# Marks, steps and relative nodes of two edge chunks in PSUM, and a pair's three lists joined by one reduction

## The chip, the cores and the metric

The kernel runs on one core of a Trainium2 chip. The metric is the device time of one execution in microseconds (us). The kernel before takes 1126.28 us, the median of three runs (1125.23 to 1130.48).

## What is computed

A layer of a graph network on 12,500 nodes with 128 features and 400,000 edges. The edges come sorted by their destination `dst`; the sources are random. An edge that is longer than 10 contributes nothing (`cut` is 0 there), and `edge_weight` is scaled so that most edges are longer. The reference, cut to what matters:

```python
rbf = exp(-(distances[:, None] - centers) ** 2 / (2 * width * width))       # 50 centers
cut = 0.5 * (cos(pi * distances / CUTOFF) + 1) * (distances <= CUTOFF)
W = (silu(rbf @ fw1 + fb1) @ fw2 + fb2) * cut[:, None]
messages = (h[src] @ pw + pb) * W
agg = segment_sum(messages, dst, num_segments=num_atoms)
y = h + (silu(agg @ mw1 + mb1) @ mw2 + mb2)
return layernorm(x + y)
```

## The kernel before

The engines are named as in the profile: PE multiplies matrices, DVE and ACT work on tiles, POOL issues the indirect DMAs (gathers and scatters by index), SP issues the plain DMAs.

**The kept edges are packed first.** The edges are cut into seven chunks; chunk c has 128 partitions with `ROWS[c]` edges each (309, 256, then 512). `pack_first` (chunk 0) and `pack(c)` (L660, the others) move each partition's kept edges to the front. For a chunk, `pack` does this on DVE:
- L671 takes the first destination of each partition, L677 marks the edges that are dropped (`drop`), a scan counts the marks along the partition (`gone`), and `step` is that count at the kept edges: by so many places each must move.
- `nodes` puts step, relative destination (`rel`, L713 or L725) and source into one 32-bit word. `spans` (L701, with L703 and L705) finds the largest relative destination. `rank` (L692, with the products L695 and L696) has PE add up the counts of the partitions before.
- For each bit of the largest step, `moving`, `resting` and `shift` (L491, L495, L485) move the edges whose step has that bit: first the words, then the lengths `r_d`.
- `columns` (L434) writes what is kept as lines, and POOL scatters them into a list in DRAM (`packed`, L470). Ahead of the fifth bit step, from chunk 2 on, SP loads the rows of the next chunk (`load_rows`, L174 to L181).

From chunk 3 on (`FROM_BANK`, `late_c`) marks, steps and relative nodes take turns in one PSUM bank, `aside`. For chunks 1 and 2 they are three tiles in SBUF, and the marks' scan takes them as both of its inputs.

**Then the list is unpacked.** Neighbouring partitions write into three different lists, so that they do not collide at their ends. `unpack(c)` (L778) loads the three into `pair`, with two 32-bit words for an edge in turn (word 0 the nodes, word 1 the length). `one_of` (L804 to L807) makes one list of the three, 256 edges wide, with two ORs: once for the nodes, once for the lengths, so 14 times in all. At a given place at most one of the three lists is not zero; chunks 0 and 1 have two more lists, which `alike_in` (L800) ORs in ahead. From the joined list come the sources of the gathers (`srci`, L874), the columns (`dl`) and the cut (`cut`); the lengths go to DRAM (`near_d`).

**The main loop** (L1463) works on quads of 512 kept edges, 139 of them. `fetch` (L1009) gathers four times 128 rows of the projected nodes `proj` by `srci` with L1015 on POOL, ahead of their use, into a ring of buffers; eight quads take their first 128 rows in single copies by SP (`one_by_one`, L992 to L1005). `basis`, `first`, `silu` and `second` (L1065 to L1082) compute the weights of the edges on ACT and PE; `message` (L1086, L1093) multiplies gathered rows and weights on DVE; `place` (L1100, L1105) makes a one-hot operand with the cut in it; `sum_up` (L1117, L1125) sums over the edges on PE into the PSUM tile "sums" (two buffers); `add` (L1144, L1148) adds the sum into the table `aggT` at its base. The node part (up to L1232) runs on the finished end of the table and after the loop.

**The order of the work** is written out when the program is built. `pack` and `unpack` are generators: each `yield` gives the modelled cost of what was just issued, and `go_on` and `pack_until` (L1360 to L1376) put packing steps between the quads while the sum of these costs, `clock[0]`, allows it. `fetches` does the same for the gathers. So a `yield` that changes can move instructions behind or ahead of others on every engine. The two costs used are

```python
def one(n):
    return 0.14 + 0.00112 * n
def two_a_cycle(n):
    return 0.13 + 0.0006 * n
```

Of the kernel before, what the change touches and what calls it, by code (L numbers as in the profile page):

```python
# [20 lines left out]
P = 128  # L21
# [4 lines left out]
W = 128  # L26
# [5 lines left out]
SB = 14  # L32
# [48 lines left out]
def kernel(  # L81
# [37 lines left out]
    nc = tc.nc  # L119
# [17 lines left out]
    ps = ctx.enter_context(tc.tile_pool(name="ps", bufs=2, space=PSUM))  # L137
# [114 lines left out]
    ones = keep.tile([P, P], F32, name="ones")  # L252
# [129 lines left out]
    LB = RB + SB  # L382
# [277 lines left out]
    def pack(c):  # L660

        R, CAP = ROWS[c], CAPS[c]
        bits = (R - 1).bit_length()

        def rowed(dt, name, n=R, bufs=1):
            return work.tile([P, max(n, R_MAX) if n == R else max(CAPS)], dt, name=name,
                             bufs=bufs)[:, :n]

        r_d, r_dst, r_src = raw[c]
        first = work.tile([P, 1], F32, name="first")  # L670
        nc.vector.tensor_copy(first, r_dst[:, 0:1])  # L671
        late_c = c >= FROM_BANK
        if late_c:
            aside = bank(c)
            held.append(c)
        drop = aside[:, :R] if late_c else rowed(F32, "drop")
        nc.vector.tensor_scalar(drop, r_d.bitcast(F32), CUTOFF, None, op0=OP.is_gt)  # L677
        yield (one(R) if late_c else two_a_cycle(R)) + 0.1
        gone = rowed(F32, "gone")
        if late_c:  # L680
            nc.vector.tensor_tensor_scan(gone, drop, ones[:, 0:1].to_broadcast([P, R]), 0.0,
                                         op0=OP.add, op1=OP.mult)
        else:
            nc.vector.tensor_tensor_scan(gone, drop, drop, 0.0, op0=OP.add, op1=OP.max)
        yield one(2 * R)
        nc.vector.tensor_scalar(cnt[:, c:c + 1], gone[:, R - 1:R], -1.0, float(R),
                                op0=OP.mult, op1=OP.add)
        step = aside.bitcast(I32)[:, :R] if late_c else rowed(I32, "step")
        nc.vector.scalar_tensor_tensor(step, drop, 0.0, gone, op0=OP.is_equal, op1=OP.mult)
        yield one(R) + 0.1  # L690

        def rank():  # L692
            at = bank()
            held.append(c)
            nc.tensor.matmul(at[:, 0:1], before, cnt[:, c:c + 1], start=True, stop=False)  # L695
            nc.tensor.matmul(at[:, 0:1], ones, run, start=False, stop=True)  # L696
            return at

        nodes = rowed(I32, "nodes", bufs=2)

        def spans():  # L701
            relc = rowed(F32, "drop")
            nc.vector.tensor_scalar(relc, rel, -127.5, None, op0=OP.add)  # L703
            yield two_a_cycle(R)
            nc.vector.tensor_reduce(span[:, c:c + 1], relc, AX.X, OP.max, apply_absolute_value=True)  # L705
            yield one(R)

        if late_c:
            nc.vector.scalar_tensor_tensor(nodes, step, LB, r_src, op0=OP.logical_shift_left,
                                           op1=OP.bitwise_or)  # L710
            yield one(R)
            rel = aside.bitcast(I32)[:, :R]
            nc.vector.tensor_scalar(rel, r_dst, first, None, op0=OP.subtract)  # L713
            yield one(R)
            nc.vector.scalar_tensor_tensor(nodes, rel, SB, nodes, op0=OP.logical_shift_left,
                                           op1=OP.bitwise_or)
            yield one(R)
            yield from spans()
            held.remove(c)
            free.append(aside)  # L720
            at = rank()
        else:
            at = rank()
            rel = rowed(I32, "rel")
            nc.vector.tensor_scalar(rel, r_dst, first, None, op0=OP.subtract)  # L725
            yield two_a_cycle(R)
            yield from spans()
            nc.vector.scalar_tensor_tensor(nodes, rel, SB, r_src, op0=OP.logical_shift_left,
                                           op1=OP.bitwise_or)
            yield one(R)  # L730
            nc.vector.scalar_tensor_tensor(nodes, step, LB, nodes, op0=OP.logical_shift_left,
                                           op1=OP.bitwise_or)
            yield one(R)
        for b in range(bits):
            if b == 4 and 1 < c < NC_ - 1:
                load_rows(c + 1)
            if b == (1 if late_c else 0):
                if 3 not in side_of:
                    sides(3, nc.vector)
                    yield 0.6  # L740
                at_i = place_at(at, side_of[3])
                nc.vector.tensor_add(run, run, cnt[:, c:c + 1])
                held.remove(c)
                free.append(at)
                yield 0.4
# [24 lines left out]
            yield one(n)  # L770

        yield from columns(c, nodes, r_d, first, 0, CAP, at_i)
        awake[c] = pool[0] + (2.2 if c == 1 else 3.0)
        awake[0] = 0.0
        yield 0
        yield from unpack(c)

    def unpack(c):  # L778
# [5 lines left out]
        np_ = p1 - p0  # L784
        pair = work.tile([64, 3, 512], I32, name="pair", bufs=1)
# [17 lines left out]

        def one_of(to, k):  # L804

            nc.vector.tensor_tensor(to, pair[:np_, 0, k::2], pair[:np_, 1, k::2], OP.bitwise_or)
            nc.vector.tensor_tensor(to, to, pair[:np_, 2, k::2], OP.bitwise_or)  # L807

        if c < 2:
            alike_in(0)  # L810
# [11 lines left out]
        two = paired(I32, "two")  # L822
# [834 lines left out]
```

## Time and profile before

| | |
|---|---|
| median of 3 runs | 1126.28 us (1125.23 to 1130.48) |
| the profiled execution | 1136.76 us |
| its span in the profile | 1134.8 us |
| granted PE clock, mean | 0.761 of full speed |
| PE busy, matmuls | 657.0 us (58%) |
| DVE busy | 582.2 us (51%), 1755 instructions |
| POOL busy | 531.7 us (47%) |
| ACT busy | 399.8 us (35%) |
| DMA | 91.38 MB, 81 GB/s over the span |

The span is the time from the first to the last recorded instruction, and 2 us of the profiled execution lie around it. A row of instructions gives their busy time, the mean of one, and the idle time of the engine just ahead of them with what ended it; "quad<-proj,srci" are the tiles written and read, and x407 the count. In lists of waits, the three numbers are the idle time in us, how often, and the longest. A minimum, median and maximum of one instruction stand as a/b/c in ns. In a timeline each row has its start and length in us, and in the bracket the engine's idle time ahead of it and what ended that. A table by stretches gives the busy time of each engine between two moments.

### The profile page before, as it was taken

What the parts mean: (1) busy time and instruction counts of PE and PEld (TensorE: products, weight loads), DVE (VectorE), ACT (ScalarE), POOL (GpSimd) and SP (SyncE); (2) the same over time, 40 slices, a digit from 0 to 9 for tenths busy, and PEclk for the clock granted to TensorE, in tenths of its full rate; (3) what the DMA queues carried; (4) which work ended last, traced back from release to release, by engine and by line L of the source; (5) the groups of instructions that cost most, each with busy time, mean ns of one, the idle gap of its engine ahead of it and who ended that gap; (6) DMA issues with size and microseconds to landing.
All of it is one profiled execution on the core that took longest, in us unless ns stands there. A gap on an engine that the chain in (4) does not pass through costs nothing. (4 is left out here: it accounts for less than half of the span.)

```text
span 1134.8 us, 13638 instructions
## 1 busy us (share of the span) xinstructions
PE 657.0 (58%) x3531; PEld 509.4 (45%) x3531; DVE 582.2 (51%) x1755; ACT 399.8 (35%) x569; POOL 531.7 (47%) x569
## 2 busy tenths in 40 slices
PE   4574337507724577125856557579266667776685
PEld 4463226406513455114645435457145455554464
DVE  8355409514723476135957557348035344444476
ACT  3344213105412245003525423156035234324565
POOL 7434732464274524745061465552745565565400
PEclk8776657858866788557987769589568778788798
DMA  6572231122121222212121223223223222322322
GB/s 213 178 234 79 72 103 39 40 83 68 57 55 44 61 73 70 63 30 68 58 75 39 64 82 92 58 69 107 62 61 98 80 69 61 113 73 76 115 61 78
DMA packets 53104, 91.38 MB, mean 81 GB/s; under 512 B 13824, under 2 KB 20576, under 8 KB 53018
## 3 DMA queue, kind: packets, MB, share of 16 engines
q1 hardware_dynamic: 34610, 53.34, 14.6%
q0 software_dynamic: 17840, 36.77, 12.4%
q8 instruction: 30, 0.49, 0.2%
q14 instruction: 56, 0.46, 0.1%
q10 hardware_dynamic: 568, 0.33, 0.1%
HBM read 74.59 MB, written 15.79 MB: 80 GB/s over the span
## 5 line engine op out<-in xcount | busy, mean ns | idle before, releaser
L1015 POOL DMA_INDIRECT quad<-proj,srci x407 | 387.2, 951 | 329.0 <-DVE msg L1093 116.4
L1082 PEld LDWEIGHTS bank<-fw_sb,s 128*128 128x128 f32 x1112 | 170.9, 218 | 138.8 <-issue 129.8
L1065 PE MATMUL ph<-rbf,w_sb 102*128 102x512 f32 x278 | 167.6, 731 | 91.7 <-ACT s L1071 52.2
L1105 DVE TENSOR_SCALAR hot<-iota_n,dl,cut 128x80 f32<-128x80 f32 (+4 forms) x408 | 110.1, 332 | 206.9 <-remote 110.5
L1071 ACT ACTIVATE s<-ph 128x1024 f32<-128x1024 f32 x70 | 71.3, 1018 | 359.5 <-remote 222.4
L1082 PE MATMUL bank<-fw_sb,s 128*128 128x128 f32 x1112 | 172.9, 302 | 34.9 <-issue 34.9
L1125 PEld LDWEIGHTS sums<-hot,msg 128*128 128x128 f32 x816 | 121.4, 215 | 96.4 <-issue 84.5
L1125 PE MATMUL sums<-hot,msg 128*128 128x80 f32 (+4 forms) x816 | 122.8, 294 | 52.0 <-issue 48.5
L1065 PEld LDWEIGHTS ph<-rbf,w_sb 102*128 102x128 f32 x278 | 57.9, 231 | 142.6 <-issue 74.9
L1079 PE MATMUL bank<-fb_b,ones_b 96*128 96x512 bf16 x139 | 59.1, 425 | 92.6 <-DVE msg L1093 37.8
L1015 POOL DMA_INDIRECT x<-proj,srci x93 | 88.1, 947 | 46.6 <-issue 27.4
L1148 DVE TENSOR_TENSOR aggT<-aggT,sums 128x80 f32 (+4 forms) x209 | 54.0, 258 | 100.4 <-remote 56.4
L327 PEld LDWEIGHTS bank<-pw_sb,xT 128*128 128x128 f32 (+1 forms) x292 | 47.9, 234 | 90.0 <-issue 71.4
L1056 ACT ACTIVATE rbf<-d,rbf_bias,rbf_scale 102x512 f32<-102x512 f32 x70 | 56.3, 804 | 70.2 <-DMA d<-near_d 60.9
L1093 DVE TENSOR_TENSOR msg<-bank,quad 128x512 f32<-128x512 f32 x78 | 52.9, 679 | 34.7 <-remote 24.6
L470 POOL DMA_INDIRECT packed<-line,at_i x7 | 7.0, 996 | 127.4 <-DVE first L671 75.1
L1015 POOL DMA_INDIRECT quad<-in_x_dram,srci x48 | 46.2, 963 | 43.4 <-DMA r_dst<-in_dst_dram 15.7
L324 PE MATMUL bank<-pb_b,ones_b 96*128 96x512 bf16 (+2 forms) x38 | 17.2, 452 | 81.7 <-ACT xT L951 62.9
L1125 PE MATMUL sums<-quad,quad 128*128 128x128 f32 (+3 forms) x296 | 44.8, 290 | 15.6 <-issue 14.9
L951 ACT COPY xT<-bank 128x512 f32<-128x512 f32 (+1 forms) x37 | 21.4, 579 | 91.5 <-remote 76.9
L327 PE MATMUL bank<-pw_sb,xT 128*128 128x128 f32 (+1 forms) x292 | 48.8, 320 | 4.2 <-ACT xT L951 4.2
L1125 PEld LDWEIGHTS sums<-quad,quad 128*128 128x128 f32 x296 | 40.7, 207 | 17.8 <-issue 16.3
(273 smaller groups left out, 920.8 us busy)
## 6 DMA issues: line engine op xcount, KB each, us to landing
d<-near_d SPq DMA_DIRECT2D x70, 256.0 KB
dl<-proj SPq DMA_DIRECT2D x1024, 0.5 KB
x<-in_x_dram SPq DMA_DIRECT2D x46, 256.0 KB
quad<-proj,srci POOLq DMA_INDIRECT x407
proj<-hp SPq DMA_DIRECT2D x24, 256.0 KB
out_dram<-x SPq DMA_DIRECT2D x22, 256.0 KB
x<-proj,srci POOLq DMA_INDIRECT x93
r_d<-in_edge_weight_dram SPq DMA_DIRECT2D x5, 256.0 KB
```

What stands on the lines that cost most here:

```text
L327: nc.tensor.matmul(to[:m, k, :], lT[:, k * P:k * P + m], w, start=False, stop=(k == a + c - 1))
L951: nc.scalar.copy(xT[:, :n], xp[:, :n])
L1015: nc.gpsimd.indirect_dma_start(out=got[:, j, :], out_offset=None, in_=proj if table is None else table, in_offset=bass.IndirectOffsetOnAxi ...
L1056: nc.scalar.activation(rbf[:u], d[:u], AF.Square, bias=rbf_bias[:u], scale=rbf_scale[:u])
L1065: nc.tensor.matmul(ph[:, h, :], w1_sb[:2 * KR, h, :], rbf[:2 * KR], start=True, stop=True)
L1071: nc.scalar.activation(s[:, :n], ph[:, :n], AF.Silu)
L1079: nc.tensor.matmul(pu, ones_b[:, :P], bias_b["fb2"].rearrange("k j f -> k (j f)"), start=True, stop=False)
L1082: nc.tensor.matmul(pu[:, j * H:(j + 1) * H], s[:, j * P:(j + 1) * P], fw2_sb, start=False, stop=(j == QT - 1))
L1093: nc.vector.tensor_mul(msg[:, a:b, :], pu_of[q].rearrange("p (j f) -> p j f", j=QT)[:, a:b, :], got_of[q][:, a:b, :])
L1105: nc.vector.tensor_scalar(hot[:, j, :wide(q)], iota_n[:, :wide(q)], dl[:, at[0], at[1]], cut[:, at[0], at[1]], op0=OP.is_equal, op1=OP.mult)
L1125: nc.tensor.matmul(pa[:, k * W:k * W + wide(q)], msg[:, j, :], hot[:, j, :wide(q)], start=(j % n == 0), stop=(j % n == n - 1))
L1148: nc.vector.tensor_add(to, to, pa[:, k * W:k * W + wide(q)])
```

## The change

Two edits, one on `pack`, one on `one_of`:
- For chunks 1 and 2 `aside` is a buffer of the PSUM tile "sums" (in their time the main loop has not begun to use it; the assertion says so). Marks, steps and relative nodes of all chunks from 1 on now live in `aside`, one after the other, and all take the order that the late chunks had: the words get the steps first, then `rel` is made over the steps and joined in, then `spans`. For chunks 1 and 2 `rank` is still requested ahead of these. The scan takes a broadcast one as its second input for all of them. The modelled cost of the marks' and of `rel`'s step grows from `two_a_cycle(R)` to `one(R)`.
- `one_of` is one reduction by exclusive or along the three lists, in place of two ORs: the view is turned so that the innermost axis runs over the lists.

```diff
@@ pack
+        else:
+            assert "two" not in pa_of
+            aside = ps.tile([P, 2, 2 * W], F32, name="sums", bufs=2).rearrange("p a w -> p (a w)")
-        drop = aside[:, :R] if late_c else rowed(F32, "drop")
+        drop = aside[:, :R]
         nc.vector.tensor_scalar(drop, r_d.bitcast(F32), CUTOFF, None, op0=OP.is_gt)
-        yield (one(R) if late_c else two_a_cycle(R)) + 0.1
+        yield one(R) + 0.1
...
-            nc.vector.tensor_tensor_scan(gone, drop, drop, 0.0, op0=OP.add, op1=OP.max)
+        nc.vector.tensor_tensor_scan(gone, drop, ones[:, 0:1].to_broadcast([P, R]), 0.0,
+                                     op0=OP.add, op1=OP.mult)
...
-        step = aside.bitcast(I32)[:, :R] if late_c else rowed(I32, "step")
+        step = aside.bitcast(I32)[:, :R]
...
+        if not late_c:
+            at = rank()
+        nc.vector.scalar_tensor_tensor(nodes, step, LB, r_src, op0=OP.logical_shift_left,
+                                       op1=OP.bitwise_or)
+        yield one(R)
+        rel = aside.bitcast(I32)[:, :R]
+        nc.vector.tensor_scalar(rel, r_dst, first, None, op0=OP.subtract)
+        yield one(R)
+        nc.vector.scalar_tensor_tensor(nodes, rel, SB, nodes, op0=OP.logical_shift_left,
+                                       op1=OP.bitwise_or)
+        yield one(R)
+        yield from spans()
         if late_c:
...
-        else:
-            at = rank()
-            rel = rowed(I32, "rel")
-            nc.vector.tensor_scalar(rel, r_dst, first, None, op0=OP.subtract)
-            yield two_a_cycle(R)
-            yield from spans()
-            nc.vector.scalar_tensor_tensor(nodes, rel, SB, r_src, op0=OP.logical_shift_left,
-                                           op1=OP.bitwise_or)
-            yield one(R)
-            nc.vector.scalar_tensor_tensor(nodes, step, LB, nodes, op0=OP.logical_shift_left,
-                                           op1=OP.bitwise_or)
-            yield one(R)
@@ one_of
-            nc.vector.tensor_tensor(to, pair[:np_, 0, k::2], pair[:np_, 1, k::2], OP.bitwise_or)
-            nc.vector.tensor_tensor(to, to, pair[:np_, 2, k::2], OP.bitwise_or)
+            nc.vector.tensor_reduce(to, pair[:np_, :, k::2].rearrange("p s e -> p e s"), AX.X,
+                                    OP.bitwise_xor)
```

More of the change, by code (lines that the diff above doesn't have):

```diff
@@ L675, in pack @@
             held.append(c)
-        drop = aside[:, :R] if late_c else rowed(F32, "drop")
+        else:
+            assert "two" not in pa_of
+            aside = ps.tile([P, 2, 2 * W], F32, name="sums", bufs=2).rearrange("p a w -> p (a w)")
+        drop = aside[:, :R]
         nc.vector.tensor_scalar(drop, r_d.bitcast(F32), CUTOFF, None, op0=OP.is_gt)
-        yield (one(R) if late_c else two_a_cycle(R)) + 0.1
+        yield one(R) + 0.1
         gone = rowed(F32, "gone")
-        if late_c:
-            nc.vector.tensor_tensor_scan(gone, drop, ones[:, 0:1].to_broadcast([P, R]), 0.0,
-                                         op0=OP.add, op1=OP.mult)
-        else:
-            nc.vector.tensor_tensor_scan(gone, drop, drop, 0.0, op0=OP.add, op1=OP.max)
+        nc.vector.tensor_tensor_scan(gone, drop, ones[:, 0:1].to_broadcast([P, R]), 0.0,
+                                     op0=OP.add, op1=OP.mult)
         yield one(2 * R)
@@ L706, in spans @@
             yield one(R)
-        if late_c:
-            nc.vector.scalar_tensor_tensor(nodes, step, LB, r_src, op0=OP.logical_shift_left,
-                                           op1=OP.bitwise_or)
-            yield one(R)
-            rel = aside.bitcast(I32)[:, :R]
-            nc.vector.tensor_scalar(rel, r_dst, first, None, op0=OP.subtract)
-            yield one(R)
-            nc.vector.scalar_tensor_tensor(nodes, rel, SB, nodes, op0=OP.logical_shift_left,
-                                           op1=OP.bitwise_or)
-            yield one(R)
-            yield from spans()
+        if not late_c:
[10 more added lines that the diff above has]
+        yield from spans()
+        if late_c:
             held.remove(c)
@@ L721, in pack @@
             at = rank()
-        else:
-            at = rank()
-            rel = rowed(I32, "rel")
-            nc.vector.tensor_scalar(rel, r_dst, first, None, op0=OP.subtract)
-            yield two_a_cycle(R)
-            yield from spans()
-            nc.vector.scalar_tensor_tensor(nodes, rel, SB, r_src, op0=OP.logical_shift_left,
-                                           op1=OP.bitwise_or)
-            yield one(R)
-            nc.vector.scalar_tensor_tensor(nodes, step, LB, nodes, op0=OP.logical_shift_left,
-                                           op1=OP.bitwise_or)
-            yield one(R)
         for b in range(bits):
```

## The prediction

> **What bounds the kernel now.** I read the page first, then the list of waits, then the busy time by stretches, and last the timelines of the stretches in which the change works. "POOL gather" is one L1015 instruction: it fetches 128 rows by index.
>
> ```profile
> span 1134.8 us, 13638 instructions
> ...
> L1015 POOL DMA_INDIRECT quad<-proj,srci x407 | 387.2, 951 | 329.0 <-DVE msg L1093 116.4
> ```
> ```profile
> POOL quad L1015 <- DVE msg L1093: 116.4, 17, 24.7
> ...
> POOL packed L470 <- DVE first L671: 75.1, 3, 35.6
> ```
> ```profile
> core 0: us, PE busy (x) PEld busy (x) DVE busy (x) ACT busy (x) POOL busy (x), PEclk, DMA share, GB/s
> 122.00:158.00 36.00, 2.97 (x13) 2.41 (x12) 8.47 (x17) 2.02 (x4) 23.88 (x26) 0.55 0.28 80
> 158.00:190.00 32.00, 25.04 (x130) 20.04 (x129) 20.89 (x55) 12.15 (x17) 0.90 (x1) 0.73 0.13 43
> 411.00:438.00 27.00, 23.29 (x147) 18.75 (x146) 24.83 (x73) 19.35 (x26) 0.42 (x2) 0.94 0.13 43
> 450.00:495.00 45.00, 7.07 (x21) 5.05 (x20) 4.26 (x11) 1.90 (x2) 33.11 (x35) 0.54 0.24 65
> ```
>
> No engine is busy all the time; two kinds of stretch alternate. In a **burst** (122 to 158, 450 to 495) POOL gathers without a pause and the others nearly stand: PE works 7.07 us of 45, DVE 4.26. Between bursts (158 to 190, 411 to 438) POOL stands, and PE and DVE work; DVE is the fuller one in the second, 24.83 us of 27. POOL stands for one of two things, as the waits say: for a DVE message (L1093), which frees the buffer that the next gather fills, or for DVE to finish the list of a chunk, which POOL then sends with L470. (The list names the instruction after the list's last one, L671.) So DVE's work counts where POOL waits for it, and is nearly free inside a burst; a gather counts inside a burst, and is free while POOL waits.
>
> ```profile
> 116.24 0.95 POOL L1015 DMA_INDIRECT x<-proj,srci  x1 [0.30 <-issue]
> ...
> 189.10 1.00 POOL L470 DMA_INDIRECT packed<-line,at_i  x1 [35.61 <-DVE first L671]
> ...
> 437.61 0.99 POOL L470 DMA_INDIRECT packed<-line,at_i  x1 [26.58 <-DVE first L671]
> ...
> 506.50 0.95 POOL L1015 DMA_INDIRECT x<-proj,srci  x1 [12.82 <-DVE msg L1093]
> ...
> 528.10 1.01 POOL L1015 DMA_INDIRECT quad<-proj,srci  x1 [6.88 <-DVE hot L1105]
> ```
> In these POOL rows the bracket is POOL's idle time and what ended it.
>
> **The change, part by part.** The sums are made against the profiled execution: 1136.76 us with a span of 1134.8, 10.5 us over the median 1126.28 of the runs shown. All terms are small, so I carry their sum in microseconds to the median.
>
> *Marks, relative nodes and spans of chunks 1 and 2.* Three instructions a chunk get an operand in PSUM: L677, L725 and L703. Chunks 3 to 6 already work so (tile "bank", 512 wide), so the trace has both forms. Numbers are minimum/median/maximum in ns; in L677 and L703 the minimum of "drop" is chunk 1 (256 wide), the maximum chunk 2 (512).
>
> ```profile
> L677 DVE TENSOR_SCALAR bank<-r_d x4: 683/684/686, 188.8 to 572.7; 128x512 f32<-128x512 f32 x4
> L677 DVE TENSOR_SCALAR drop<-r_d x2: 293/354/416, 49.4 to 100.2; 128x256 f32<-128x256 f32 x1, 128x512 f32<-128x512 f32 x1
> L713 DVE TENSOR_SCALAR bank<-r_dst,first x4: 747/750/754, 192.3 to 592.0; 128x512 int32<-128x512 int32 x4
> L725 DVE TENSOR_SCALAR rel<-r_dst,first x2: 476/478/480, 50.8 to 102.6; 128x256 int32<-128x256 int32 x1, 128x512 int32<-128x512 int32 x1
> L703 DVE TENSOR_SCALAR drop<-bank x4: 675/680/684, 195.3 to 593.3; 128x512 f32<-128x512 int32 x4
> L703 DVE TENSOR_SCALAR drop<-rel x2: 293/360/428, 51.4 to 103.1; 128x256 f32<-128x256 int32 x1, 128x512 f32<-128x512 int32 x1
> ```
> Chunk 2 pays 684 - 416, 750 - 480 and 680 - 428 ns: 0.27 + 0.27 + 0.25 = **0.8 us**. Its other instructions only change order. Chunk 1 is half as wide and pays at most half, 0.4 us, which is covered: DVE then stands for 13.65 us.
>
> ```profile
> 68.44 0.22 DVE L479 TENSOR_SCALAR at_f<-bank,end 128x1 f32<-128x1 f32 x1 [13.65 <-ACT xT L951]
> ...
> 115.64 0.18 DVE L874 CAST srci<-bank 128x44 int32<-128x44 f32 x1
> ...
> 188.53 0.29 DVE L462 TENSOR_TENSOR line<-r_d,there 128x136 int32<-128x136 int32 x1
> ```
> Chunk 2 has no such cover. Its preparation stands in DVE's queue ahead of the indices of chunk 1 (L874 at 115.64, landed at 115.82), and POOL's gather at 116.24 follows them by 0.4 us with only its usual 0.30 of pause; behind the burst the list ends at 188.53 and POOL sends at 189.10. I take the whole 0.8.
>
> *The lists of a pair (L806, L807): 14 times two ORs of 256 become one reduction of 768.* This is the unknown. The ORs stand 213.73 to 214.63: 0.90 us for a list.
>
> ```profile
> 213.73 0.41 DVE L806 TENSOR_TENSOR two<-pair 44x256 int32<-44x256 int32 x1
> 214.18 0.42 DVE L807 TENSOR_TENSOR two<-two,pair 44x256 int32<-44x256 int32 x1
> 214.63 0.29 DVE L825 TENSOR_SCALAR part<-two 44x256 int32<-44x256 int32 x1
> ```
> ```profile
> L705 DVE TENSOR_REDUCE span<-drop x6: 421/680/687, 51.7 to 601.6; 128x1 f32<-128x512 f32 x5, 128x1 f32<-128x256 f32 x1
> L709 DVE SCALAR_TENSOR_TENSOR nodes<-bank,r_src x4: 677/692/692, 191.6 to 577.0; 128x512 int32<-128x512 int32 x4
> L1178 DVE SCALAR_TENSOR_TENSOR zs<-zt,bank x20: 1043/1072/1100, 678.1 to 1087.7; 128x512 f32<-128x512 f32 x20
> ```
> The only reduction in the trace takes 421 ns for 256 elements and 680 for 512: 1.01 ns an element and 162 ns fixed. 768 elements would be 0.94 us, with the 0.04 pause of these rows 0.98: **+0.08 a list**. But the new one reads with a jump at every element, from list to list. L1178 steps over its elements too (every fourth) and takes 1072 ns where the contiguous L709 takes 692: (1072 - 162) / 512 = 1.78 ns an element, so 1.37 + 0.16 + 0.04 = 1.57: **+0.67 a list**. A gain I exclude: nothing here reduces faster than 1.01 ns an element. I take +0.08, because L705 is the same operation with one input, while L1178 reads two; the other end is a rival.
>
> The Trainium skill, page "Vector Engine (DVE) Microarchitecture Reference", section "5.2 Measured stream behaviour on trn2", speaks on both sides: an operation with one source hopping at every element took 1.73 ns a column, yet a one-source operation alternating between two regions kept the full rate. By the first figure a list would be an estimated 1.53 us (768 x 1.73 + 162 + 40 ns), +0.63; L1178's 1.78 agrees with it, and no row here shows a reduction that hops.
>
> How many lists count? Those of chunks 0 to 2 stand right ahead of the indices that POOL needs; those of chunk 4 end at 505.6, where the message stands that releases POOL at 506.50; 3 and 5 lie likewise between bursts. I count 12 of 14: **+1.0 us**.
>
> *The order.* The writer of the order adds up modelled costs, and these grow. Against before, DVE's chunk instructions slip by one behind messages from chunk 1's indices on, until the lists of chunk 3 are packed. One r_d step of chunk 2 (128x504, 0.6 us from start to start) leaves a burst for the stretch that ends at 188.53, and one node step of chunk 3 does the same in the next: **+1.2 us**. PE's only move: chunk 2's rank product goes behind one more transpose and product. POOL's: the sends of chunks 4 and 5 go behind one more gather. That gather now runs while POOL stands (26.58 us ahead of 437.61) and not in the burst behind. A gather comes every 1.25 us (the step from 0.95 and 0.30 in the rows): **-2.5 us** for two, if the bursts keep their length otherwise.
>
> ```profile
> 106.10 0.28 PE L695 MATMUL bank<-cnt,before 128*128 128x1 f32 x2
> ...
> 107.16 1.05 PE L327 MATMUL bank<-pw_sb,xT 128*128 128x128 f32 x8
> ```
> ```profile
> 107.59 0.20 DVE L479 TENSOR_SCALAR at_f<-bank,end 128x1 f32<-128x1 f32 x1
> ```
> The rank would end near 108.2, where the L327 group ends; DVE's reader at 107.59 comes 0.8 later itself, so it waits 0.1 at most; without its own delay it would wait 0.6. Queued behind it are chunk 2's steps.
>
> ```profile
> 234.76 0.69 SPq L181 DMA_DIRECT2D r_d<-in_edge_weight_dram  x1
> ...
> 245.34 9.02 SPq L1005 DMA_DIRECT2D dl<-proj  x7
> ```
> ```profile
> 307.24 0.15 DVE L671 CAST first<-r_dst 128x1 f32<-128x1 int32 x1
> ```
> SP: the three loads of chunk 4's rows (234.76) go behind one bias load, one distance load and seven single-row copies, some 13 us (9.02 and two more issues of about 2). They are first read at 307.24, so 50 us of cover remain; the distance load moves up by three issues.
>
> **The sum:** 0.8 + 1.0 + 1.2 - 2.5 = +0.5 us, so about **1127**.
>
> **The rivals.**
> 1. *The reduction runs at the rate of L1178.* 12 x 0.67 = 8.0 in place of 1.0: +7.5, **1134**, slower. It decides from about 1.35 us a list (12 x 0.45 = 5.4 with the other terms). For: the jump at every element, the row of L1178. Against: one input, contiguous output, and L705's rate.
> 2. *Messages come earlier, and that counts more than the steps behind them.* About a dozen messages now stand ahead of one chunk step of 0.6 to 0.7 us (L485 or L491) that preceded them. If POOL waits for just these (17 waits, 116.4 us in all), 12 x 0.65 = 7.8 us come off, less 2.5, plus the 1.8 of preparation and lists: -8.5, **1118**, faster. Against: the steps are only put off, and the next list is late by what was put off.
> 3. *It doesn't show.* The added DVE time falls into the bursts, where DVE stands anyway (4.26 of 45 us busy), and the two gathers only lengthen POOL's next wait: 0, **1126**. For: POOL also waits for the one-hot operands (6.88 us at 528.10), for PE's sake, and these don't care.
>
> **How the numbers follow.** Forecast 0.48, rival 1 0.22, rival 2 0.17, rival 3 0.13. A measurement of this kernel can tell about 0.5% from no change: 5.6 us, so "same" is 1120.6 to 1131.9. Rival 2 gives faster, with 0.01 from the forecast's tail: 0.18. Forecast and rival 3 give same, less that and 0.06 for lists between the two rates: 0.54. Rival 1 and the 0.06 give slower: 0.28. The range goes from rival 2's 1118 to 1136, two past rival 1, for lists that all count. The forecast's own range is 1122 to 1132.
>
> **What the profile after would show.** L806 as a reduction: 0.94 us confirms the forecast, 1.5 rival 1. L677, L713 and L703 in chunk 2 at 0.68, 0.75 and 0.68. POOL's sends near 190.5 and 439, with eight gathers ahead of the second where there were seven. Bursts behind the sends of chunks 4 and 5 shorter by one gather. If bursts begin or end elsewhere by several microseconds, the order decides and not the durations, and my sum is wrong whatever its terms.

## The result, and the profile after

The changed kernel takes 1143.31 us, the median of six runs (1137.30 to 1147.38); beside it the kernel before took 1131.09 us (six runs, 1125.23 to 1142.22). The ratio is **1.012**, with a 95% interval of 1.008 to 1.016: some 13.6 us slower (the medians lie 12.2 us apart). The forecast of +0.5 us was wrong, and 1143.31 lies outside the range of 1118 to 1136. On some chips both kernels take some 1130 us, on others some 730 us, so every ratio below compares runs of one chip, and it leaves out executions more than 1.5% above the fastest of their kernel, which the medians count.

The two profiled executions don't show the loss: after's was its fastest run (1137.30 us, span 1135.2), before's (1136.76) lay 5.7 us above before's median. What one execution shows in a stretch is therefore compared over several kernels of the same order, in the table further down. What single instructions cost, the profile after does show. It has its own line numbers: behind L735 those of before less 10 (L1005 is the gather, L1083 the message, L1095 the one-hot, L1115 the sum, L925 the `f_cut` of before's L935).

First the rows of DVE by line, in ns as before ("sums" is the new place), then the timeline at chunk 3's list (start, length in us):

```profile
L680 DVE TENSOR_SCALAR sums<-r_d x2: 418/550/683, 48.9 to 99.5; 128x256 f32<-128x256 f32 x1, 128x512 f32<-128x512 f32 x1
L703 DVE TENSOR_SCALAR drop<-sums x2: 414/544/674, 51.9 to 106.6; 128x256 f32<-128x256 int32 x1, 128x512 f32<-128x512 int32 x1
L796 DVE TENSOR_REDUCE two<-pair x6: 1256/1258/1264, 111.6 to 709.8; 44x256 int32<-44x768 int32 x2, 46x256 int32<-46x768 int32 x2, 22x256 int32<-22x768 int32 x1, 54x256 int32<-54x768 int32 x1
```
```profile
103.57 0.75 DVE L714 TENSOR_SCALAR sums<-r_dst,first 128x512 int32<-128x512 int32 x1
...
210.66 1.26 DVE L796 TENSOR_REDUCE two<-pair 44x256 int32<-44x768 int32 x1
211.95 0.28 DVE L815 TENSOR_SCALAR part<-two 44x256 int32<-44x256 int32 x1
```

Chunk 2's three instructions in PSUM take 683, 750 and 674 ns, as taken from the late chunks. The reduction takes 1.26 us, and a list 1.29 from start to start (210.66 to 211.95) where the two ORs took 0.90: **+0.39 a list**, between the 0.08 of the forecast and the 0.67 of rival 1.

The Trainium skill, page "Vector Engine (DVE) Microarchitecture Reference", section "5.2 Measured stream behaviour on trn2", gives 1.73 ns a column for a source that hops at every element, and the full rate for one stream that alternates between two regions. Neither agrees here: with the 162 ns fixed that the prediction took from L705, (1258 - 162) / 768 is 1.43 ns an element.

Then POOL's rows of after, to be set beside those of before at 189.10 and 437.61:

```profile
186.85 1.00 POOL L470 DMA_INDIRECT packed<-line,at_i  x1 [32.81 <-DVE first L671]
...
248.83 0.94 POOL L1005 DMA_INDIRECT quad<-proj,srci  x1 [7.27 <-DVE msg L1083]
...
258.99 0.94 POOL L1005 DMA_INDIRECT quad<-proj,srci  x1 [5.46 <-ACT s L1061]
...
280.02 0.94 POOL L1005 DMA_INDIRECT quad<-proj,srci  x1 [6.35 <-DVE msg L1083]
...
305.42 1.00 POOL L470 DMA_INDIRECT packed<-line,at_i  x1 [16.95 <-DVE first L671]
...
437.86 0.99 POOL L470 DMA_INDIRECT packed<-line,at_i  x1 [26.47 <-DVE first L671]
```
```profile
263.88 0.95 POOL L1015 DMA_INDIRECT quad<-proj,srci  x1 [13.32 <-DVE msg L1093]
...
270.30 0.99 POOL L1015 DMA_INDIRECT quad<-proj,srci  x1 [1.73 <-DVE msg L1093]
...
291.22 0.99 POOL L1015 DMA_INDIRECT x<-proj,srci  x1 [6.07 <-DMA dl<-proj]
...
307.60 1.00 POOL L470 DMA_INDIRECT packed<-line,at_i  x1 [12.89 <-DVE first L671]
```

The second fence is before. Each row but the sends starts a burst; in between the gathers follow at 1.25 us. Ahead of chunk 3's send (the last row of before, the one at 305.42 of after) before's last three bursts hold 4, 12 and 3 gathers, and POOL then waits 12.89 us for the list. After's last two hold the same 19 gathers as 12 and 7 (the four at 248.83 are those that before issues at 245.86), and it waits 16.95. This is so in every profile of a chip of this kind: 12 and 7 in all five kernels with the order of after in this stretch, 4, 12 and 3 in all five with that of before.

### The profile page after: what moved, and what is told of

Its sections match the earlier page's. It is cut to its first block, busy times and chain, and to the rows that moved or that the text cites. A ratio compares the mean times of both kernels' runs of the same rounds, so it can differ in the third digit from the quotient of the medians.

```text
span 1135.2 us, 13626 instructions
## 1 busy us (share of the span) xinstructions
PE 673.7 (59%) x3531; PEld 519.7 (46%) x3531; DVE 588.0 (52%) x1741; ACT 399.4 (35%) x569; POOL 531.3 (47%) x569
## 3 DMA queue, kind: packets, MB, share of 16 engines
q0 software_dynamic: 17840, 36.77, 12.5%
## 5 line engine op out<-in xcount | busy, mean ns | idle before, releaser
L1005 POOL DMA_INDIRECT quad<-proj,srci x407 | 387.3, 952 | 335.4 <-DVE msg L1083 120.5
L1072 PEld LDWEIGHTS bank<-fw_sb,s 128*128 128x128 f32 x1112 | 177.1, 224 | 162.3 <-issue 154.0
L1055 PE MATMUL ph<-rbf,w_sb 102*128 102x512 f32 x278 | 174.3, 759 | 94.7 <-ACT s L1061 79.5
L1095 DVE TENSOR_SCALAR hot<-iota_n,dl,cut 128x80 f32<-128x80 f32 (+4 forms) x408 | 109.4, 332 | 226.0 <-remote 109.3
L1072 PE MATMUL bank<-fw_sb,s 128*128 128x128 f32 x1112 | 181.2, 309 | 54.4 <-issue 54.3
L1115 PEld LDWEIGHTS sums<-hot,msg 128*128 128x128 f32 x816 | 123.8, 219 | 88.3 <-issue 73.9
L1115 PE MATMUL sums<-hot,msg 128*128 128x80 f32 (+4 forms) x816 | 124.6, 298 | 42.0 <-issue 37.3
L1055 PEld LDWEIGHTS ph<-rbf,w_sb 102*128 102x128 f32 x278 | 60.8, 243 | 146.9 <-ACT s L1061 83.4
L1005 POOL DMA_INDIRECT x<-proj,srci x93 | 88.2, 948 | 42.7 <-issue 27.4
L1005 POOL DMA_INDIRECT quad<-in_x_dram,srci x48 | 46.2, 962 | 42.6 <-PE bank L696 14.2
L1083 DVE TENSOR_TENSOR msg<-bank,quad 128x512 f32<-128x512 f32 x78 | 53.0, 679 | 11.8 <-remote 11.4
L327 PE MATMUL bank<-pw_sb,xT 128*128 128x128 f32 (+1 forms) x292 | 51.1, 331 | 5.1 <-issue 4.6
L1115 PE MATMUL sums<-quad,quad 128*128 128x128 f32 (+3 forms) x296 | 44.3, 289 | 16.3 <-issue 14.8
L1083 DVE TENSOR_TENSOR quad<-bank,quad 128x512 f32<-128x512 f32 (+2 forms) x40 | 25.1, 632 | 51.4 <-remote 27.9
L1115 PEld LDWEIGHTS sums<-quad,quad 128*128 128x128 f32 x296 | 40.7, 208 | 16.9 <-issue 14.6
```

What stands on the lines that cost most here:

```text
L327: nc.tensor.matmul(to[:m, k, :], lT[:, k * P:k * P + m], w, start=False, stop=(k == a + c - 1))
L1005: nc.gpsimd.indirect_dma_start(out=got[:, j, :], out_offset=None, in_=proj if table is None else table, in_offset=bass.IndirectOffsetOnAxi ...
L1055: nc.tensor.matmul(ph[:, h, :], w1_sb[:2 * KR, h, :], rbf[:2 * KR], start=True, stop=True)
L1072: nc.tensor.matmul(pu[:, j * H:(j + 1) * H], s[:, j * P:(j + 1) * P], fw2_sb, start=False, stop=(j == QT - 1))
L1083: nc.vector.tensor_mul(msg[:, a:b, :], pu_of[q].rearrange("p (j f) -> p j f", j=QT)[:, a:b, :], got_of[q][:, a:b, :])
L1095: nc.vector.tensor_scalar(hot[:, j, :wide(q)], iota_n[:, :wide(q)], dl[:, at[0], at[1]], cut[:, at[0], at[1]], op0=OP.is_equal, op1=OP.mult)
```

## The experiments

**Theory A**: the modelled costs of the raised yields (the order) and the slower lists each cost what they cost alone, and add; PSUM operands cost little. **Rivals**: B, the order alone carries it; C, delays of the lists grow through the bursts; D, PSUM operands cost 3 us or more; E, it needs order and lists together.

### Lists, PSUM and order taken apart

The lists alone: before with only this edit, which leaves the order of all engines as it was.

```diff
-            nc.vector.tensor_tensor(to, pair[:np_, 0, k::2], pair[:np_, 1, k::2], OP.bitwise_or)
-            nc.vector.tensor_tensor(to, to, pair[:np_, 2, k::2], OP.bitwise_or)
+            nc.vector.tensor_reduce(to, pair[:np_, :, k::2].rearrange("p s e -> p e s"), AX.X,
+                                    OP.bitwise_xor)
```


> Before with the reduction alone: every instruction stands in the order of before, with 14 reductions in place of 28 ORs. In the profile after, a list takes 1.30 us from start to start (1.26 busy) where the two ORs took 0.90. Theory A (the price of the lists carries the slowdown, each on the path): 14 x 0.40 = 5.6 us over before, ratio about 1.005, and the shift of the order explains the rest. Theory B (the shift of the order carries it; lists fall where POOL does not wait): 0 to 2 us, ratio 1.000 to 1.002. Theory C (delays add up through the bursts to more than their own length): over 8 us, ratio 1.008 or more.

Measured: 1133.26 us against 1128.22, ratio 1.0047 (95% interval 1.0011 to 1.0084): 5.3 us (1.2 to 9.5).

PSUM and order without the lists: after with this edit turned back.

> After with the two ORs put back: PSUM operands and the shifted order, no reduction. Theory A: after less 5.6 us, so about 1.007 of before. Theory B: as after, about 1.011 of before. Theory C: close to before, 1.000 to 1.004.

Measured: 1136.58 us, 1.0096 (1.0052 to 1.0140): 10.8 us (5.9 to 15.8).

The order alone: before with only the two costs raised.

```diff
-        yield (one(R) if late_c else two_a_cycle(R)) + 0.1
+        yield one(R) + 0.1
...
             nc.vector.tensor_scalar(rel, r_dst, first, None, op0=OP.subtract)
-            yield two_a_cycle(R)
+            yield one(R)
```


> Before with only the modelled costs of the two steps raised (one(R) for two_a_cycle(R)): PE, ACT, POOL and SP have exactly the order of after, DVE too but for the instructions that the change rewrites; marks, steps and relative nodes stay in SBUF and the ORs stay. Theory A: the order costs what the lists leave, about 8 us, ratio 1.007; if PSUM costs its 1.2 us of added DVE time, 1.006. Theory B: nearly all of the slowdown, 1.010 or more. Theory C: 1.000 to 1.003.

Measured: 1136.88 us, 1.0064 (1.0023 to 1.0106): 7.2 us (2.6 to 12.0). It has the instructions and operands of before; only their order differs.

The changed kernel beside them:

> The changed kernel once more beside the three others on one chip. All theories: 1.008 to 1.016 of before, as measured before; if it comes out within 0.5% of before, the measured slowdown hangs on the chip or on the run and not on the kernel.

Measured: 1141.02 us, 1.0111 (1.0070 to 1.0153): 12.5 us, the sum of 5.3 and 7.2. The other pair of parts adds up less well: with PSUM and order at 10.8, only 1.7 would be left for the lists. Each part is uncertain by 4 to 5 us, so neither sum proves that the parts simply add. The same cut the other way round, after with the costs of before:

```diff
-        yield one(R) + 0.1
+        yield (one(R) if late_c else two_a_cycle(R)) + 0.1
...
         nc.vector.tensor_scalar(rel, r_dst, first, None, op0=OP.subtract)
-        yield one(R)
+        yield one(R) if late_c else two_a_cycle(R)
```


> After with the modelled costs of before for the two steps: all operands in PSUM and the reductions as in after, but PE, ACT, POOL and SP have exactly the order of before, and DVE too but for the instructions rewritten. Theory A (order and lists each cost what they cost alone, and add): 1133 to 1134 us, 1.005 of before, the 5 us of the lists and at most 1.2 for PSUM. Theory D (PSUM operands cost 3 to 4 us): 1.008. Theory E (the slowdown needs both, order alone is chance): 1.000 to 1.003 or as after, 1.011.

Measured: 1135.40 us against 1133.20, a difference of 2.2 by the medians, and 1.0112 (1.0031 to 1.0193) by the ratio. On this chip before's times lie between 1114.62 and 1149.53. The interval holds a value of each theory, so it tells nothing. With the ORs put back as well, so that PSUM alone is left:

> Before with marks, steps and relative nodes of chunks 1 and 2 in PSUM alone: the order of before, the two ORs, the costs of before. Theory A: 0 to 1.2 us, ratio 1.000 to 1.001. Theory D: 1.003 or more.

Measured: 1128.35 us, 1.0018 (0.9971 to 1.0066): PSUM costs 2 us at -3 to +7 by the ratio, and by the medians nothing (1128.35 is below 1133.20). So D isn't excluded by it. The rows speak against D: longer instructions make 0.8 us in chunk 2. The 10.8 us with PSUM against the 7.2 without speak for it, within their intervals. D stays open.

What follows: C falls, since the kernel without the reductions lies at 1.0052 or more, where C gave 1.004 at most; the 5.3 us of the lists are also just what they are longer (14 x 0.39 = 5.5). E falls, since lists and order each cost something alone, clear of zero. B gave the lists 0 to 2 us; the interval from 1.2 touches that, so B is unlikely and not excluded. Theory A fits best. By the middle values the order is its larger term, which the intervals leave open.

### Where the order costs: chunk 3's stretch

The order of after up to a send, then that of before: the modelled clock is set back there. The edit stands in `columns`, ahead of the send, in the kernel with raised costs alone; c is 2 in the first kernel and 3 in the second.

```diff
+        if c == 2:
+            clock[0] += -0.84
         fetches(clock[0] + (4.0, 5.0, 5)[min(c, 2)], most[0])
         sent.add(c)
```


> The order of after only up to the send of chunk 2's list: raised costs, and the modelled clock set back by 0.84 us at that send, so that POOL and SP keep the order of before throughout, and DVE that of after for chunks 1 and 2 only. SBUF and ORs as in before. Theory A, part 1 (the loss lies in chunk 3's stretch, where the wait ahead of its send is 17 us instead of 13 to 14): 0 to 1 us, ratio 1.000 to 1.001, and that wait stays at 13 to 14 us. Rival (the loss lies in chunks 1 and 2): 1.004 or more.

> The order of after up to the send of chunk 3's list, that of before behind it (clock set back by 0.84 us there): the sends of chunks 4 and 5 and POOL's order are those of before. Theory A, part 1: the wait ahead of chunk 3's send is 17 us, and the kernel 3.5 to 4 us slower than before, 1.003; what is left to 1.0064 to 1.0075 belongs to the sends of chunks 4 and 5 and SP's order. Rival: all of the 1.0064 to 1.0075, or nothing.

Measured: 1129.63 and 1132.40 us, ratios 1.0056 (1.0008 to 1.0104) and 1.0059 (1.0011 to 1.0107). The first is not at the 1.000 to 1.001 that was expected, and the ratios agree with its rival (1.004 or more); by the medians, on the other hand, neither kernel is slower than before (1133.20). The totals on this chip don't settle where the order costs. The stretches of the profiles are clearer. In us, from the rows of the seven sends (0 to 6) of each kernel; "wait" is POOL's ahead of send 3:

| kernel | order up to send 3 | lists | sends 0 to 2 | 2 to 3 | wait | 3 to 6 | 6 to end |
|---|---|---|---|---|---|---|---|
| before | before | OR | 145.2 | 118.5 | 12.9 | 385.5 | 441.6 |
| reduction alone | before | reduction | 142.4 | 115.0 | 13.8 | 389.8 | 440.2 |
| after, old costs | before | reduction | 143.0 | 116.3 | 14.5 | 388.5 | 437.6 |
| order of after to send 2 | before from send 2 | OR | 143.3 | 114.2 | 13.0 | 383.1 | 439.6 |
| order of after to send 3 | after | OR | 142.5 | 123.3 | 17.0 | 389.8 | 435.7 |
| costs alone | after | OR | 142.3 | 119.5 | 17.1 | 386.0 | 442.4 |
| after with ORs | after | OR | 143.3 | 119.0 | 17.1 | 385.9 | 436.2 |
| after, beside them | after | reduction | 142.5 | 119.1 | 17.2 | 389.0 | 444.8 |
| after | after | reduction | 142.6 | 118.6 | 17.0 | 390.5 | 439.3 |

From send 2 to send 3 the order makes 119.9 of 116.0 (means of five and of four): **+3.9 us**, and the lists nothing that can be seen. Something else spreads this stretch under either order. In before and in the kernel with the order of after to send 3, a burst of 20 gathers runs into the next four after 1.24 and 2.17 us, and POOL stands 13.32 and 14.61 us behind them. Without these two the means are 119.05 (118.6 to 119.5) and 115.17 (114.2 to 116.3), the same +3.9, and the two groups don't overlap.

From send 3 to 6 the kernels with the reduction take 389.5, those with the ORs 386.1 (four and five): **+3.4** for the lists, and nothing for the order. But the five with the ORs lie between 383.1 and 389.8, so this is not clear of the scatter. The kernel with PSUM alone is not in the table, since its profiled execution (1137.77 us) lay 9.4 us above its median; its bursts are 4, 12 and 3 and its wait 14.6 us, as before's order has them, and from send 3 to 6 it took 392.0 with the ORs. Behind send 6 single executions lie between 436 and 445, whatever the kernel; what is left of the 12.5 us can't be placed there by one profile each.

The mechanism, as two kernels show it that differ in the order between send 2 and send 3. POOL of the first, then of the second:

```profile
258.51 0.95 POOL L1017 DMA_INDIRECT quad<-proj,srci  x1 [2.23 <-DVE msg L1095]
...
265.60 0.99 POOL L1017 DMA_INDIRECT quad<-proj,srci  x1 [2.38 <-DVE msg L1095]
...
286.42 0.98 POOL L1017 DMA_INDIRECT x<-proj,srci  x1 [6.04 <-DVE msg L1095]
```
```profile
265.23 0.95 POOL L1017 DMA_INDIRECT quad<-proj,srci  x1 [14.61 <-ACT s L1073]
...
286.28 0.99 POOL L1017 DMA_INDIRECT quad<-proj,srci  x1 [6.34 <-DVE msg L1095]
...
311.76 1.00 POOL L472 DMA_INDIRECT packed<-line,at_i  x1 [16.98 <-DVE first L673]
```

The bursts are 4, 12 and 3 gathers in the first, 12 and 7 in the second, with the same 19 gathers in them. A burst makes the other engines nearly stand some 8 us after it begins. In after the one that begins at 258.99 does it: from 266.88 on, PE issues single products. DVE is caught at a one-hot, one message earlier than in before, and the four gathers which that message frees come only in the next burst. DVE and PE of after:

```profile
263.21 0.67 DVE L1083 TENSOR_TENSOR msg<-bank,quad 128x512 f32<-128x512 f32 x1
276.05 0.97 DVE L1095 TENSOR_SCALAR hot<-iota_n,dl,cut 128x56 f32<-128x56 f32 x4 [12.17 <-remote]
...
279.08 0.68 DVE L1083 TENSOR_TENSOR msg<-bank,quad 128x512 f32<-128x512 f32 x1
...
302.39 0.98 DVE L1095 TENSOR_SCALAR hot<-iota_n,dl,cut 128x56 f32<-128x56 f32 x4 [3.39 <-PE sums L1115]
```
```profile
266.88 0.27 PE L1072 MATMUL bank<-fw_sb,s 128*128 128x128 f32 x1 [0.26 <-issue]
269.00 0.27 PE L1072 MATMUL bank<-fw_sb,s 128*128 128x128 f32 x1 [1.85 <-issue]
270.39 0.27 PE L1072 MATMUL bank<-fw_sb,s 128*128 128x128 f32 x1 [1.12 <-issue]
271.81 0.37 PE L1072 MATMUL bank<-fw_sb,s 128*128 128x128 f32 x1 [1.15 <-issue]
...
286.97 1.05 PE L1072 MATMUL bank<-fw_sb,s 128*128 128x128 f32 x8
287.87 1.00 PE L1115 MATMUL sums<-hot,msg 128*128 128x56 f32 x8
291.55 0.44 PE L859 MATMUL bank<-ident,f_cut 44*128 44x44 f32 x2 [2.69 <-DVE f_cut L925]
293.34 0.58 PE L1069 MATMUL bank<-fb_b,ones_b 96*128 96x512 bf16 x1 [1.35 <-DVE msg L1083]
293.72 1.91 PE L1072 MATMUL bank<-fw_sb,s 128*128 128x128 f32 x8
...
299.14 3.05 PE L1055 MATMUL ph<-rbf,w_sb 102*128 102x512 f32 x4
302.02 1.00 PE L1115 MATMUL sums<-hot,msg 128*128 128x56 f32 x8
```

The burst of 7 (280.02 to 288.5) lasts long enough to slow the engines once more: PE waits 2.69 us for the `f_cut` behind the one-hots and 1.35 for a message. Then eight L1072 take 1.91 us in place of 1.05, and full speed is back by 302.02. DVE's last steps of the list wait behind a one-hot for PE's sums (3.39 us at 302.39). All five profiles with this order have both waits of PE here, of 2.47 to 2.69 and 1.35 to 1.44 us, and the slow products behind them; in none of the five with before's order does PE wait for the `f_cut`. In the kernel with bursts of 4, 12 and 3 the same place looks so:

```profile
291.79 1.00 PE L1127 MATMUL sums<-hot,msg 128*128 128x56 f32 x8
292.71 0.32 PE L871 MATMUL bank<-ident,f_cut 44*128 44x44 f32 x2
293.13 0.38 PE L1081 MATMUL bank<-fb_b,ones_b 96*128 96x512 bf16 x1
293.35 1.05 PE L1084 MATMUL bank<-fw_sb,s 128*128 128x128 f32 x8
```

No wait, and 1.05 us. In after the granted clock is 0.50 from 291.5 to 301 and 1.00 from 302 on. The Trainium skill, page "TensorE: Matmul & The Clock Gate", Part 1, has the array's clock halve after an idle window of about 3.4 us and come back after one of sustained work. The size of the step agrees (1.05 and 1.91 us, 1.00 and 0.50). The times don't: the clock fell in the idle time of 2.69 us, and it came back some 8 us after steady work began at 293.34.

Which of chunk 3's slipped steps does it was to be told by two kernels that set the clock back at bit step 3 and at bit step 6:

```diff
+            if c == 3 and b == 3:
+                clock[0] -= 0.84
             n, k = reach(c, b, bits), 1 << b
```


> The order of after up to chunk 3's bit step 3 (the words by 508 places' reach), that of before from there on: modelled clock set back by 0.84 us at that step. Theory A, part 1, sharpened (bit steps 3 to 5 behind the messages let these come earlier; gathers run together into a burst that begins earlier, the engines stand earlier in it, the message that should free the next buffer misses it, and its four gathers fall into a second burst): the wait ahead of chunk 3's send is 13 to 14.6 us and gathers 123 to 134 form one burst as before; 0 to 1 us over before. Rival (any slip of chunk 3's steps costs it, or the last steps do): 17 us as in after if the early steps do it.

> As the kernel beside it, but with the clock set back at bit step 6: the two differ only in five DVE steps of chunk 3 (bits 3 to 5), which here stand one message later. Theory A, part 1, sharpened: the wait ahead of chunk 3's send is 17 us, 3.5 to 4 us over its neighbour. Rival (the slip of the last steps, ahead of the send, costs it): 13 to 14.6 us.

They ran on a chip of the other kind: 729.96 and 730.86 us against 729.54, ratios 1.0004 (0.9983 to 1.0026) and 1.0015 (0.9994 to 1.0036), with a wait of 0.30 us ahead of send 3 in both. There the question doesn't arise, and it stays open. Both were run twice more:

> The kernel with the order of after up to chunk 3's bit step 3, once more for its profile. On a chip on which before takes over 1100 us: wait ahead of chunk 3's send 13 to 14.6 us by theory A, part 1, sharpened; 17 us by the rival. On a chip on which before takes 730 us the wait is under 1 us by both.

> The kernel with the order of after up to chunk 3's bit step 6, once more for its profile. On a chip on which before takes over 1100 us: wait ahead of chunk 3's send 17 us by theory A, part 1, sharpened; 13 to 14.6 us by the rival. On a chip on which before takes 730 us the wait is under 1 us by both.

> The kernel with the order of after up to chunk 3's bit step 3, a third time for its profile, in case this chip is one on which before takes over 1100 us: there the wait ahead of chunk 3's send is 13 to 14.6 us by theory A, part 1, sharpened, 17 us by the rival. Where before takes 730 us it tells nothing.

> The kernel with the order of after up to chunk 3's bit step 6, a third time for its profile, for the same reason: wait ahead of chunk 3's send 17 us by theory A, part 1, sharpened, 13 to 14.6 us by the rival, where before takes over 1100 us.

Measured: 728.29 and 729.34 us against 729.12, then 731.88 and 732.12 against 730.58, one run each; again a chip of that kind both times.

The sends of chunks 4 and 5 alone: the order of before up to send 3, then the clock set forward (`if c == 3: clock[0] += 0.84` at the same place in before).

> The order of before up to the send of chunk 3's list, and behind it POOL's order of after (clock set forward by 0.84 us there): the sends of chunks 4 and 5 stand one gather later, four DVE steps of chunk 4 one message later. Theory A, part 2 (as the prediction had it, a gather out of the burst behind each send): 2.5 us faster than before, 0.998, and the stretch between the sends of chunks 5 and 6 at 122 us instead of 125. Rival (the sends one gather later cost, by the list that comes 1.25 us later): 1.002 or more.

Measured, again on such a chip: 729.79 us, 1.0002 (0.9984 to 1.0020). Neither the 2.5 us of gain nor a loss.

On chips of the first kind the two gathers moved just as forecast. In the four profiles with POOL's order of after, the bursts ahead of the sends of chunks 4 and 5 hold 8 gathers in place of 7, and those behind them 43 in place of 44 and 19 in place of 20. The rows of after, then of before, whose burst of 7 begins at 528.10:

```profile
527.79 1.01 POOL L1005 DMA_INDIRECT quad<-proj,srci  x1 [6.89 <-DVE hot L1095]
...
571.79 0.99 POOL L470 DMA_INDIRECT packed<-line,at_i  x1 [34.22 <-DVE line L462]
```
```profile
570.63 0.99 POOL L470 DMA_INDIRECT packed<-line,at_i  x1 [33.97 <-DVE line L462]
```

Behind send 4, the gathers that begin near 506 start 1.3 us sooner after the send with the ORs (67.6 against 68.9, two kernels each; in a third with before's order these gathers are split in two) and 1.4 sooner with the reduction (68.4 against 69.8): the length of one gather is gained. But from the start of the burst ahead of send 5 to that send it takes 44.0 to 45.5 us with eight gathers (mean of four 44.7), and 42.5 to 42.8 with seven (mean of five 42.6). So the list is 2.1 us later there, by the eighth gather or by the DVE steps that move with it, which no run separates.

### How many lists count, and what the change costs where the engines don't stand

Before with three reductions in place of the two ORs of each list (the second and third give the same list again):

```diff
+            for _ in range(3):
+                nc.vector.tensor_reduce(to, pair[:np_, :, k::2].rearrange("p s e -> p e s"), AX.X,
+                                        OP.bitwise_xor)
```


> The order of before with every reduction done three times (the second and third give the same list): 28 more instructions of 1.25 us, 35 us of DVE time over the kernel with the reduction alone. If 12 of 14 lists stand on the path, as the prediction counted: 30 us over that kernel, 35 over before, ratio 1.031. If the stages of the profiles are right (only the lists of chunks 4 to 6 show in them, about half): 15 to 18 us over it, 20 to 23 over before, 1.018 to 1.020. If nearly none: under 1.010.

Measured: 755.82 us against 729.54, 1.0363 (1.0336 to 1.0391): 26.5 us. Its DVE time grows by 41.6 (28 x 1.29 + 14 x 0.39), so 0.64 of it counts. Against the neighbour with the order of after up to bit 3, the profile is 22.8 us longer, and the stretches between the sends grow by 3.6, 3.6, 3.4, -0.8, 0.0 and 7.6 us, the one behind send 6 by 5.3. The two lists of a chunk are 5.9 us longer (4 x 1.29 + 2 x 0.39). So there those of chunks 0 to 2 and 6 count in part, those of 5 in full (7.6), and those of 3 and 4 don't: ten of 14, by one profile each.

> The changed kernel once more; the last four kernels ran on a chip on which before takes 729.5 us and POOL hardly waits. If this run is on such a chip: theory A gives the lists' share alone, 14 x 0.40 us x 0.65 (the share by which the three reductions lengthened the kernel: 26.3 us of 28 x 1.25 + 14 x 0.40) = 3.6 us, 0.8 for PSUM and 0 to 1 for the order, so 4 to 5.5 us, ratio 1.006 to 1.0075; the rival (the slowdown hangs on the stretches in which all engines stand) gives under 1.003. On a chip like the first ones: 1.008 to 1.016 as before.

Measured, before at 729.12: 731.35 us, 1.0021 (0.9997 to 1.0045): 1.5 us (-0.2 to +3.3). The lists alone, before at 730.58:

> The order of before with the reduction alone, once more. Where before takes 730 us: 14 x 0.40 x 0.65 = 3.6 us by the share that the three reductions showed, 1.005; if the single reduction hides where three don't, under 1.002, and then the 2 us that after costs there belong to the order and PSUM. Where before takes over 1100 us: 1.001 to 1.008 as before.

Measured: 732.37 us, 1.0020 (0.9994 to 1.0047): 1.5 us (-0.4 to +3.4). Where the engines don't stand, the change costs some 1.5 us, as much as its lists do alone, and neither is clear of zero. That is under the 4 to 5.5 that were expected, and no cost of the order can be told. By the middle values a single reduction hides better than three (1.5 of 5.5 us against 26.5 of 41.6). How different the chips are, the copies of single rows on SP show, 14 steps each, after on a chip of the first kind and of the second, both while POOL gathers:

```profile
261.68 14.86 SPq L995 DMA_DIRECT2D dl<-proj  x14
```
```profile
165.43 5.07 SPq L995 DMA_DIRECT2D dl<-proj  x14
```

And POOL's waits of after, on the first kind and on the second (total us, times, longest):

```profile
POOL quad L1005 <- DVE msg L1083: 120.5, 17, 27.6
```
```profile
POOL quad L1005 <- DVE msg L1083: 4.5, 4, 3.6
```

On the second kind POOL gathers nearly all the time, and the engines work beside it: between 200 and 300 us of after there, POOL is busy for 75.6 us with gathers that come every 1.25 us, and PE for 85.3.

## Why the prediction was wrong

- **Preparation of chunk 2, +0.8.** The durations came out as taken: from its marks to its first bit step chunk 2 took 8.71 us (99.54 to 108.25) in place of 7.80 (100.18 to 107.98). The price of PSUM in the whole kernel was measured as 2 us at -3 to +7, which neither confirms nor refutes the term.
- **The lists, +1.0.** The size of one failed: +0.39 in place of +0.08. At twelve lists that is 4.7 us, and the kernel with the lists alone measured 5.3 (1.2 to 9.5). "L705 is the same operation with one input" was the wrong reason: the jump costs also with one input, a little over half of what L1178's row gave. That twelve count fits the total; which of them do was seen only on the other kind of chip, where it was ten.
- **The order, +1.2 - 2.5.** This is the step that failed: the sum had -1.3 us for the order, and the kernel that has only the order measured +7.2 (2.6 to 12.0). The first part reads "One r_d step of chunk 2 (...) leaves a burst for the stretch that ends at 188.53, and one node step of chunk 3 does the same in the next". I priced slipped steps by their own 0.6 us. Chunk 2's cost nothing that can be seen (sends 0 to 2: 142.8 in six kernels with its order of after, 143.5 in three with before's). Chunk 3's cost 3.9 us, not by their length but since the gathers were grouped anew: one burst long enough to make the engines stand became two. Of the 7.2 us, these 3.9 are placed.
- **Two gathers ahead of the sends, -2.5.** They did move, and the bursts kept their length otherwise (43 for 44, 19 for 20). But send 3 to send 6 takes 386.0 us in the two kernels with the order of after and ORs, 386.1 in the three that have POOL's order of before there: no gain is seen. What failed is that a gather "is free while POOL waits". Behind send 4 a gather's length was gained (1.3 to 1.4 us), but the list of send 5 came 2.1 us later behind a burst of eight.
- **Rival 1** had the right sign and an instruction near its threshold (1.29 of 1.35 us). At the measured price, the sum would have been 1130.5 us (0.8 + 4.7 + 1.2 - 2.5), and it misses the rest. **Rival 2** had the right mechanism, messages that come earlier and release POOL earlier, and took it for a gain; in chunk 3 it is what merges and splits the bursts. **Rival 3** failed.
- The last sentence of the prediction named its own weak point, that a change of the bursts decides and not the durations; it had no chance of its own among the rivals.

Left open: what of the order's cost is not in chunk 3's stretch, which of its steps regroups the bursts, whether PSUM operands cost more than their 0.9 us, and why bursts make the engines stand on one kind of chip alone.

## What to carry to other kernels

A modelled cost that orders the work is part of the change: test it apart from the instruction, since here the raised cost alone lost some 7 us, no less than the slower instruction by the middle values. Where a stretch alternates between a gathering engine and the others, price a slipped step by the buffer that its message frees and the burst which that gather joins, and not by its own length. A reduction along an axis of three far apart elements was slower (1.26 us) than two ORs along the long axis (0.41 and 0.42): it steps through 768 elements where each OR steps through 256 pairs, and pays for the jump at each. Count the steps, and not the instructions.

## What the runs showed of the hardware that was not expected

- The same program takes some 1130 us on some chips and some 730 us on others, with POOL's gathers at 0.95 us on both. On the kind with 1130 us everything else nearly stands some 8 us after a burst of gathers begins (258.99 to 266.88 in after): PE issues single products 1.4 to 2.1 us apart, and 14 copies on SP take 14.86 us in place of 5.07.
- The reduction of 3 x 256 elements with a jump at each takes 1.26 us, 1.43 ns an element.
- After idle times of 2.69 and 1.35 us PE ran at a granted clock of 0.50, and full speed came back only after some 8 us of steady work (293.34 to between 301 and 302).
